# Layer 1 causal attention of a two-layer decoder: when the later-token value sums are made

## The chip, the cores and the metric

The kernel runs on one core of a Trainium2 chip. The metric is the device time of one execution in microseconds (us); the time before is 1584.54 us, the median of three runs.

## The reference, cut to what matters

A post-norm decoder of two layers works on `x` of 4 batches x 512 tokens x 512 features, in float32. Each layer is a self-attention, a cross-attention and a feed-forward, each added to `x` and layer-normalized. The change is in the self-attention of layer 1 (16 heads of 32 features):

```python
kqv = x @ Wqkv + bqkv                      # (b, s, 3, 16, 32): q, k, v
scores = einsum('bsnh,btnh->bnst', k, q) / sqrt(32)
scores = triu(scores) + -10000.0 * tril(ones, k=-1)
attn = softmax(scores, axis=2)
out = einsum('bnkq,bknh->bqnh', attn, v)
out = out @ Wo + bo
```

The masked places are not left out: the score there is -10000, not minus infinity. So each row's result is the sum over the tokens up to it, plus a factor exp(-10000 - row maximum) times the plain sum of the values of all later tokens. That plain sum depends on `v` alone, and one matrix of 128 x 512 for each of the four tiles of 128 tokens holds it for all 16 heads. These are the later-token value sums.

## The kernel before

**Stages and lanes.** Six phases are written as Python generators: A, B, C (attention, cross-attention and feed-forward of layer 0) and D, E, F (of layer 1), each for batches 0 to 3. `lanes` keeps two generators alive and steps them in turn; a generator ends a step with `yield`. A generator can say "next", after which the next one of the order A0 A1 ... F3 may start beside it. D says so at head 8 (`hh == D_NEXT`, 7), so D1 starts while D0 does heads 9 to 16. Weight preparation runs as background generators beside given stages (`BESIDE`); beside D1 to D3 this is the unpacking of the feed-forward's 4-bit codes (L1074, L1075, L1082 on VectorE, 22 tiles).

**Deferred steps.** Inside a generator, `pipe.later(n, f)` puts off `f` by n ticks, and each step begins with `pipe.tick()`. So while head `hh` has its scores made, head `hh-1` has its softmax and head `hh-2` its transposes.

**The order on the engines.** The Tile framework takes the traced program, gives each instruction a priority by its place in the code, and a planner with its own model of durations writes the queue of each engine; an instruction that is ready by that model can pass an earlier one that isn't. Semaphores and buffers are assigned by it. A buffer of a pool is given to a tile at its first write and comes back after its last reader; a tile that finds none waits.

**Pools.** `self.op` ("o") has 69 buffers of 128 x 512 float32 and holds weights, values, stacked queries and keys and most other results; `tp` ("t") has 13 for short-lived tiles; PSUM has 8 banks under one tag.

**One batch of D** (`l1_attn`), with float32 values split into a high and a low part where a product needs three passes (`mm3`, L154 to L156):
- Steps 0 to 7: load `x`, transpose it (L248) and split it into `xT` (`dxh`, `dxl`: 8 tiles of "o").
- `project(w, m)`: 12 matmuls to one bank (`dq`) give queries (w = 0) or keys (w = 1) of the four heads 4m+1 to 4m+4. `pair` evacuates (ScalarE, L840, L842), rounds (ScalarE, L844) and makes the low part (GpSimd, L845). `stack` loads four "o" tiles `stk` (L853), each with three DMAs, two from SyncE's queue and one from GpSimd's. The projections of m = 0 come before the values, the others at heads 1, 2 / 5, 6 / 9, 10.
- Four steps of values: 12 matmuls each into `dv`; `values` keeps `dv` and its two parts `dvh`, `dvl` (12 tiles of "o" in all).
- Sixteen head steps: `scores` (L908, four matmuls of one head from its two `stk`), `soft` (VectorE L919, ScalarE L923), `turn` (transposes L933, copies L942 to `dpT`), and behind every fourth head `values_out` (L953, matmuls `do` from ten `dpT` tiles) and `keep_out` (L958).
- `later_sum(i)`: for token tile i, matmuls (L894) of the constant 0/1 matrices `upto` and `after` with `dvh` and `dvl`. All four sums accumulate in one PSUM bank, from tile 3 down to tile 0; after each, `keep_sum` copies the bank to an "o" tile `suf[i]` (ScalarE, L899).
- Behind the heads: `suf[i]` is scaled (GpSimd, L989) and added to the turned outputs (VectorE, L983, L984), the result is transposed (`dF`), multiplied by `Wo` (`dy`), added and normalized.

In the code heads are counted from 0 (`hh`); the text counts them from 1. D0 to D3 are the four batches of this phase.

Of the kernel before, what the change touches and what calls it, by code (L numbers as in the profile page):

```python
# [23 lines left out]
NT = 4  # L24
# [44 lines left out]
class Net:  # L69
# [750 lines left out]
    def l1_attn(self, b):  # L820
# [11 lines left out]
        def project(w, m):  # L832
            ps = self.pa("dq")
            self.mm3(ps, [(self.cols(self.w1[k, w], slice(m * P, (m + 1) * P)), xT[k]) for k in range(NT)])
            pipe.later(1, pair, w, m, ps)
# [49 lines left out]
        def later_sum(i):  # L885


            if not later:
                later.append(self.pb("suf"))
            ps = later[0]  # L890
            todo = [(self.upto, r) for r in vp[i + 1]] if i + 1 < NT else []
            todo += [(self.after, r) for r in vp[i]]
            for n, (l, r) in enumerate(todo):
                nc.tensor.matmul(ps, l, r, start=i + 1 == NT and n == 0, stop=n == len(todo) - 1, skip_group_check=True)  # L894
            pipe.later(1, keep_sum, i, ps)
# [5 lines left out]
        def scores(hh):  # L901
            q3, k3 = st.pop((0, hh)), st.pop((1, hh))
            p01, p2, p3 = self.pa("ds"), self.pa("ds"), self.pa("ds")
            place = ((p01, 0), (p01, 256), (p2, 0), (p3, 0))
            tiles = []
            for i, (ps, o) in enumerate(place):
                w = max(256, P * (i + 1))
                nc.tensor.matmul(ps[:, o : o + w], q3[:, i * P : (i + 1) * P], k3[:, 0:w], start=True, stop=True, skip_group_check=True)  # L908
                tiles.append(ps[:, o : o + P * (i + 1)])
            pipe.later(1, soft, hh, tiles)  # L910
# [50 lines left out]
        for hh in range(16):  # L961
            pipe.tick()
            if hh % 4 < 2 and hh < 12:
                project(hh % 4, hh // 4 + 1)
            if hh < 4:
                later_sum(NT - 1 - hh)
            scores(hh)
            yield "next" if hh == D_NEXT else None
        yield from pipe.drain()
# [400 lines left out]
```

## Time and profile before

| what | value |
|---|---|
| runs | 1584.54 us median of 3 (1584.25 to 1585.16) |
| profiled execution | 1581.65 us, span 1580.0 us |
| mean granted TensorE clock | 0.996 |
| TensorE / VectorE / ScalarE / GpSimd busy | 1515.4 / 1232.9 / 1021.3 / 666.2 us |
| first and last later-sum matmul | 775.7 and 1076.4 us |

First score matmul of a head (L908; four of them belong to one head), in us from the start of the span:

| batch | head 1 | head 5 | head 9 | head 13 | head 16 |
|---|---|---|---|---|---|
| D0 | 776.1 | 792.6 | 808.0 | 821.2 | 831.5 |
| D1 | 859.3 | 878.4 | 898.0 | 918.6 | 929.0 |
| D2 | 974.6 | 993.3 | 1008.8 | 1022.7 | 1033.9 |
| D3 | 1061.5 | 1078.5 | 1097.6 | 1117.7 | 1128.1 |

How to read the profile: PE is the matmul part of TensorE, PEld its weight loads, DVE is VectorE, ACT ScalarE, POOL GpSimd, SP SyncE, and a q behind a name is that engine's queue (its sequencer). L894 is line 894 of the kernel. A row `a <- b` says that a waited and that b ended the wait. A tile is named without its number, and `out<-in` says what an instruction writes and reads. Matmuls overlap, so the busy time of PE is no measure of its work; the distance between the starts of two matmuls in a row is.

### The profile page before, as it was taken

Reading aid. Unit: us, or ns where it says so; the run is one execution under the profiler, and the core shown is the slowest. Engines: PE = TensorE matmul, PEld = TensorE weight load, DVE = VectorE, ACT = ScalarE, POOL = GpSimd, SP = SyncE. Lnnn points to the kernel's source line nnn. Section 1 sums busy time; section 2 is a strip of 40 time slices with the busy share of each in tenths; the row PEclk is TensorE's granted clock in tenths of the full one; section 3 lists DMA queues with packets and bytes.
Section 4 is the critical chain, followed back from the end, with each engine's and each line's share of the span. In section 5 each row is a group of like instructions: output and inputs, shape, how many; then the busy total and the mean of one; then the engine's idle time right before and its main releaser. Section 6 shows DMA issues by size and latency. Waiting matters only on the chain.

```text
span 1580.0 us, 25595 instructions
## 1 busy us (share of the span) xinstructions
PE 1515.4 (96%) x8222; PEld 1090.1 (69%) x8222; DVE 1232.9 (78%) x2658; ACT 1021.3 (65%) x2208; POOL 666.2 (42%) x672
## 2 busy tenths in 40 slices
PE   8999999999999999899999999999999999999996
PEld 6888786444544674477777668777687777777875
DVE  6486589999976688777577797767786888888896
ACT  5333336988878877888696864969634445545554
POOL 6673663555535303430435323353225344344342
PEclk9999999999999999999999999999999999999998
DMA  7043344455214744653434445633436630020101
GB/s 255 29 157 124 113 154 132 149 173 176 78 48 123 224 137 133 201 185 134 134 102 118 104 141 148 171 97 92 125 123 222 233 110 12 24 81 1 54 1 53
DMA packets 134150, 192.31 MB, mean 122 GB/s; under 512 B 17265, under 2 KB 52081, under 8 KB 134017
## 3 DMA queue, kind: packets, MB, share of 16 engines
q1 hardware_dynamic: 129888, 182.23, 36.3%
q0 software_dynamic: 4128, 8.46, 2.2%
q8 instruction: 65, 1.06, 0.3%
q14 instruction: 69, 0.56, 0.1%
HBM read 117.75 MB, written 47.71 MB: 105 GB/s over the span
## 4 chain that ended last, share of the span: by engine, by line
PE 63%; DVE 17%; ACT 8%; issue 6%; DMA 3%; POOL 3%; SPq 0%; ACTq 0%; DVEq 0%; POOLq 0%
PE fg L1185 7%; PE facc L1168 5%; PE dT L933 3%; DVE fg L1141 3%; PE pg L687 3%; PE had L755 2%; PE dn L741 2%; DVE bsm L474 2%; PE pu L689 2%; ACT de L923 2%; PE bo L498 2%; PE do L953 2%; PE qk L156 2%; PE qk L155 2%; PE qk L154 2%
## 5 line engine op out<-in xcount | busy, mean ns | idle before, releaser
L1141 DVE SCALAR_TENSOR_TENSOR fg<-fg,gs,fg 128x512 f32<-128x512 f32 x220 | 163.2, 745 | 30.9 <-ACT fg L1133 15.3
L923 ACT ACTIVATE de<-de,dm 128x128 f32<-128x128 f32 (+3 forms) x256 | 142.9, 563 | 11.3 <-DVE dm L919 10.9
L1185 PE MATMUL fg<-fxh,gu 128*128 128x512 f32 x352 | 140.2, 398 | 6.1 <-DVE fg L1141 3.1
L919 DVE CUSTOM_DVE_ANT_0 de<-ds,negm,thr 128x128 f32<-128x128 f32 (+3 forms) x256 | 126.4, 546 | 19.4 <-PE ds L908 16.0
L482 POOL TENSOR_SCALAR be<-be,bsm 128x512 f32<-128x512 f32 x128 | 96.5, 766 | 103.8 <-DVE bsm L480 72.7
L1185 PE MATMUL fg<-fxl,gu 128*128 128x512 f32 x352 | 137.4, 390 | 0.1
L664 POOL TENSOR_TENSOR hl<-g,hh 128x512 fp32r<-128x512 f32 x64 | 83.4, 1309 | 110.2 <-ACT hh L663 90.2
L1145 POOL TENSOR_TENSOR fg<-fg,fg 128x512 f32<-128x512 f32 x44 | 60.2, 1367 | 139.6 <-DVE fg L1141 60.0
L476 ACT ACTIVATE be<-bs,bsm 128x512 f32<-128x512 f32 x128 | 87.3, 690 | 31.1 <-DVE bsm L474 29.2
L845 POOL TENSOR_TENSOR dql<-dqf,dqh 128x512 fp32r<-128x512 f32 x32 | 41.4, 1295 | 150.8 <-ACT dqh L844 150.6
L933 PE MATMUL dT<-ident,de 128*128 128x128 f32 x640 | 92.0, 280 | 8.5 <-ACT de L923 6.4
L933 PEld LDWEIGHTS dT<-ident,de 128*128 128x128 f32 x640 | 72.3, 142 | 28.3 <-ACT de L923 14.0
L1185 PEld LDWEIGHTS fg<-fxh,gu 128*128 128x128 f32 x352 | 66.0, 188 | 30.1 <-DVE fg L1141 12.7
L474 DVE TENSOR_REDUCE bsm<-bs 128x1 f32<-128x512 f32 x128 | 83.4, 672 | 0.0
L498 PE MATMUL bo<-bpT,cT 128*64 128x512 f32 x256 | 76.7, 618 | 2.4 <-ACT bpT L489 1.2
L248 PEld LDWEIGHTS bT<-ident,be 128*128 128x128 f32 x512 | 54.9, 141 | 34.0 <-issue 11.5
L248 PE MATMUL bT<-ident,be 128*128 128x128 f32 x512 | 73.2, 281 | 3.6 <-POOL be L482 2.1
L1185 PEld LDWEIGHTS fg<-fxl,gu 128*128 128x128 f32 x352 | 66.1, 188 | 12.8 <-DVE fxl L146 0.4
L352 POOL TENSOR_TENSOR z<-z,rope_cos 128x512 f32<-128x512 f32 x32 | 46.8, 1473 | 64.8 <-DVE zs L349 57.8
L1133 ACT ACTIVATE fg<-fg,gs 128x512 f32<-128x512 f32 x88 | 60.1, 684 | 20.6 <-PE fg L1185 20.4
L687 PE MATMUL pg<-qT,tb 128*128 128x512 bf16 x256 | 66.8, 381 | 4.5 <-ACT qT L649 2.8
L1159 POOL TENSOR_TENSOR fhl<-fg,fhh 128x512 fp32r<-128x512 f32 x44 | 58.5, 1331 | 29.5 <-ACT fhh L1158 29.3
(355 smaller groups left out, 4640.3 us busy)
## 6 DMA issues: line engine op xcount, KB each, us to landing
x<-x SPq DMA_DIRECT2D x176, 256.0 KB, 3.0
had_scratch<-hw SPq DMA_DIRECT2D x64, 256.0 KB, 2.3
z<-had_scratch SPq DMA_DIRECT2D x64, 256.0 KB, 5.8
stk<-dqh SPq DMA_DIRECT2D x192, 64.0 KB, 2.1
tw<-in_wg_t SPq DMA_DIRECT2D x32, 256.0 KB, 3.8
tw<-in_wu_t SPq DMA_DIRECT2D x32, 256.0 KB, 3.7
tw<-in_wd_t SPq DMA_DIRECT2D x32, 256.0 KB, 2.8
p<-in_gu_p SPq DMA_DIRECT2D x22, 256.0 KB, 3.1
```

The costliest lines, as they stand in the source:

```text
L248: self.nc.tensor.transpose(pt[:, i * P : (i + 1) * P], srcs[i][:, j * P : (j + 1) * P], self.ident)
L474: nc.vector.tensor_reduce(sm[:, h : h + 1], ps, AX.X, ALU.max, negate=True)
L476: nc.scalar.activation(e, ps, AF.Exp, bias=sm[:, h : h + 1], accum_out=sm[:, 2 + h : 3 + h])
L482: nc.gpsimd.tensor_scalar(es[h][i], es[h][i], sm[:, 4 + h : 5 + h], 1.0, ALU.mult, ALU.mult)
L498: nc.tensor.matmul(po[0][h * 64 : h * 64 + 64, :], cT[j][:, c : c + 64], pTs[h], start=j == 0, stop=j == NT - 1)
L664: nc.gpsimd.tensor_tensor(lo, g, hi.bitcast(F32), ALU.subtract)
L687: nc.tensor.matmul(pg, tern["wg_t"][k, c][:, m], qT[k], start=k == 0, stop=k == NT - 1)
L919: nc.vector.tensor_tensor_reduce(es[i], ps, self.negm[:, 384 - P * i :], -1.0, self.thr[:, i : i + 1], ALU.add, ALU.min, n4[:, i : i + 1])
L923: nc.scalar.activation(es[i], es[i], AF.Exp, bias=n4[:, i : i + 1], scale=-1.0, accum_out=den[:, hh * 4 + i : hh * 4 + i + 1])
L933: nc.tensor.transpose(pt[:, o + (i - j) * P : o + (i - j + 1) * P], es[i][:, j * P : (j + 1) * P], self.ident)
L1141: self.emitted["DVE"] = nc.vector.scalar_tensor_tensor(y[u], ps, s, y[u], ALU.mult, ALU.add)
L1185: nc.tensor.matmul(ps, self.gu[i, u][:, g * P : (g + 1) * P], xT[g][n], start=n == 0, stop=n == 1)
```

## The change

The four calls of `later_sum` move from the steps of heads 1 to 4 to those of heads 13 to 16, in each of the four batches. The order of the four sums stays: tile 3 first, tile 0 last. The call still stands ahead of the head's `scores`.

```diff
@@ -962,8 +962,9 @@
             pipe.tick()
             if hh % 4 < 2 and hh < 12:
                 project(hh % 4, hh // 4 + 1)
-            if hh < 4:
-                later_sum(NT - 1 - hh)
+
+            if hh >= 12:
+                later_sum(15 - hh)
             scores(hh)
             yield "next" if hh == D_NEXT else None
         yield from pipe.drain()
```

## The prediction

> **What bounds the kernel now.** I read the page first, then the later sums' own instructions, then the engines' busy time in the attention heads, then SyncE's queue and the chain of waits.
>
> The page's engine line and its chain say that TensorE carries most of the kernel, but not alone:
>
> ```profile
> PE 1515.4 (96%) x8222; PEld 1090.1 (69%) x8222; DVE 1232.9 (78%) x2658; ACT 1021.3 (65%) x2208; POOL 666.2 (42%) x672
> ...
> PE 63%; DVE 17%; ACT 8%; issue 6%; DMA 3%; POOL 3%; SPq 0%; ACTq 0%; DVEq 0%; POOLq 0%
> ```
>
> These are averages over six stages. The change lives in the fourth, from about 775 to 1140 us, so it is priced there. The view of the tile `suf` gives what is moved: x16 and x12 are counts over the four batches, then min/median/max in ns.
>
> ```profile
> L894 PE MATMUL suf<-dvh,after x16: 388/393/396, 775.7 to 1076.2; 128*128 128x512 f32 x16
> L894 PE MATMUL suf<-dvl,after x16: 389/393/403, 775.9 to 1076.4; 128*128 128x512 f32 x16
> L899 ACT COPY suf<-suf x16: 568/582/601, 776.5 to 1077.3; 128x512 f32<-128x512 f32 x16
> L989 POOL TENSOR_TENSOR suf<-suf,dm x16: 1066/1084/1549, 844.4 to 1137.6; 128x512 f32<-128x512 f32 x16
> ```
>
> Next the busy time, in stretches from the first score matmul (L908) of head 1 to that of head 5, and from that of head 13 to 5 us behind that of head 16. Columns: stretch, length, then PE, PEld, DVE, ACT, POOL busy us (with counts), granted clock, DMA share, GB/s. Four rows for heads 1 to 4 of D0 to D3, then four for heads 13 to 16.
>
> ```profile
> 776.10:792.60 16.50, 15.52 (x84) 12.25 (x84) 9.60 (x35) 16.16 (x45) 6.49 (x10) 1.00 0.39 98
> 859.30:878.40 19.10, 17.15 (x90) 13.00 (x89) 16.04 (x46) 15.63 (x44) 6.43 (x10) 1.00 0.44 117
> 974.60:993.30 18.70, 18.59 (x95) 14.47 (x94) 15.07 (x49) 15.62 (x46) 6.57 (x10) 1.00 0.62 186
> 1061.50:1078.50 17.00, 16.45 (x88) 12.77 (x87) 14.69 (x45) 15.44 (x44) 6.62 (x10) 1.00 0.37 93
> 821.20:836.50 15.30, 14.68 (x109) 10.66 (x110) 14.28 (x44) 15.30 (x47) 5.01 (x4) 1.00 0.22 73
> 918.60:934.00 15.40, 13.72 (x106) 10.06 (x105) 15.35 (x53) 12.83 (x41) 0.00 (x0) 1.00 0.21 69
> 1022.70:1038.90 16.20, 14.32 (x113) 10.51 (x112) 14.77 (x45) 16.20 (x50) 5.00 (x4) 1.00 0.20 60
> 1117.70:1133.10 15.40, 13.87 (x106) 10.09 (x105) 13.84 (x49) 13.06 (x41) 0.00 (x0) 0.98 0.02 5
> ```
>
> The reader is to see that the last four heads are not free. In D0 and D2 ScalarE is busy without a gap there (15.30 of 15.30, 16.20 of 16.20); in D1 VectorE is (15.35 of 15.40). TensorE alone has room.
>
> Last, what SyncE's queue waits for in batch D1 (858 to 940 us; total, times, longest), and then the chain of waits there (start, length, what):
>
> ```profile
> SPq L853 <- PE do L953: 10.8, 1, 10.8
> ```
>
> ```profile
> 884.31 2.29 PE do L953 x32
> ```
>
> L853 loads the stacked queries and keys of heads to come. Its next load is issued at 885.32, after 10.8 us of waiting, just behind the first value matmuls (`do`, L953) of heads 1 to 4 at 884.31. Those read the transposed probabilities `dpT`, and with them ten buffers of the pool "o" come free. So the loads wait for buffers.
>
> **The change part by part.**
>
> *What moves.* For each batch 2+4+4+4 = 14 matmuls and 4 ScalarE copies. Successive L894 rows of the timeline start 0.23 us apart (775.69, 775.92), so 14 x 0.23 = 3.2 us of TensorE; 4 x 0.582 = 2.3 us of ScalarE. Nothing is added, no DMA moves, and SyncE and GpSimd get no new instruction. One PSUM bank is held during heads 13 to 16 instead of 1 to 4.
>
> *Heads 1 to 4, relieved.* In D0 ScalarE is 16.16 of 16.50 busy, so its 2.3 us come off. In D1 ten of the 14 matmuls stand in gapless TensorE stretches (860.9 to 867 and 874.6 to 878.4), 10 x 0.23 = 2.3. In D2 (TensorE 18.59 of 18.70) and D3 (ScalarE 15.44, TensorE 16.45 of 17.00) I take 2.3 too; a batch's bounds are 1 and 3.2. Sum: -9.2 (-4 to -12.8).
>
> *Heads 13 to 16, loaded.* In D0 and D2 the four copies go to a full ScalarE: +2.3 each (bounds 0, if other copies fall back behind VectorE, and 3.2). The matmuls fit in TensorE's gaps there. In D1 VectorE is full and gets nothing; TensorE runs without a gap only in heads 13 and 14, where 2+4 matmuls cost 6 x 0.23 = 1.4 (0 to 3.2). In D3 nothing runs beside the tail: the same 1.4, plus the two copies of heads 15 and 16, 1.2, in a chain that is ScalarE's exponentials from 1127 to 1132 us: 2.6 (0 to 5.5). Sum: 2.3 + 2.3 + 1.4 + 2.6 = +8.6 (0 to 15).
>
> So the move itself is a swap, -0.6 us.
>
> [...]
>
> *New waits.* All four sums share a bank, so each waits for the copy of the one before. Before, TensorE and its loads waited 2.6 us in 7 times for that. Behind such a matmul stands the next head's score group, for which VectorE and then ScalarE wait. With ScalarE full its copy comes later, but one head keeps ScalarE 3.8 us (15.3/4) while scores and first reduction take about 1 us (0.65 + 0.35), so it should not starve: 0 taken, up to +3 in all. GpSimd's L989 now reads sums that are made last; the earliest of D0 runs at 844.4, while D0's last scores are out by 834. The copy of sum 0 is due about one head later (3.8 us), so 6 us cover it; GpSimd's additions, splits and stack loads for the next batch queue behind it if not.
>
> *The pool "o", 69 buffers.* This is the term that decides. Today the eight tiles `dvh`, `dvl` end in heads 1 to 4, and four `suf` tiles begin. After the change all eight live on to heads 13 to 16 and no `suf` exists until then: from head 4 to 13 four buffers more are held. I count who holds one in D1 at 881.5 us, just ahead of the first value matmuls, from first write to last read in the trace: 32 weight pairs and 1 bias, 8 of `xT`, 4 of `v`, 4 `suf`, 6 stacks still unread, 10 `dpT`, 4 `do` of D0's merge = 69. It is exactly full. With 73 wanted, the value matmuls, which need all ten `dpT`, must wait until four buffers come back; the score matmuls give two a head, so for two heads' scores, of which today one is out in time (883.2) and the next comes 4.5 us later (887.6). What then is late: the stack loads of heads 9 to 12 behind it on SyncE (16 issues, 885.3 to 895.4) and D0's `dF` splits.
>
> How much of that is paid? Later scores can be drawn forward, so nothing is a floor (a gain has no reason: buffers only get fewer); twice a head's 4.5 us is the ceiling, 9. The nearest row is what the full pool costs already. By the usual spacing of each shape (0.226 us for 512 columns, 0.109 for 128, 0.072 for L953) TensorE's work in heads 5 to 8 is 16.4 us of D1's 19.6 and 14.7 of D0's 15.4. D1 idles about 3.3 us; I take as much again: +3.3. D0 and D2 have no merge beside heads 1 to 4; the same count reaches 69 in head 5, and four more overflow for some 3 us, mostly stacks with 4 us to spare: +0.4 each (0 to 2). In D3 eight weight buffers are free already (63 at most): 0. Sum: +4.1 (0 to 13).
>
> [...]
>
> **The sum.** -9.2 + 8.6 + 4.1 = +3.5 us. The profiled execution took 1581.65 us (span 1580.0 and 1.65 around it), 2.9 below the median of the runs; the terms are differences, so I put them on the median: 1584.54 + 3.5 = 1588.0. About 0.2%, 3.2 us, is what a measurement of this kernel can tell from no change.
>
> **The rivals.**
> - *The cover holds* (faster). If the last heads' ScalarE is elastic and the planner draws scores forward so that the pool never stalls TensorE, the relief of 9.2 meets only D1's and D3's 4.0: -5 us, 1579.5. For it: TensorE's gaps in heads 13 to 16. Against it: ScalarE without one gap in D0 and D2. It decides if the late copies cost less than half (under 2.3 of 4.6) and D1's heads 5 to 8 stay at 19.6 us.
> - *Nothing nets* (same). The planner orders by its own idea of ready; the moved matmuls depend only on the values, and if it pulls them forward into gaps they end early and free the pool. Then the change does not quite do what it says: about +0.5, 1585. For it: L894 already wanders by a group in the timeline (in the middle of a projection at 875.9). Against: TensorE's order follows the code almost everywhere in these heads.
> - *The pool at its ceiling* (slower). Both value groups of D1 stall, 9 us, and D0 and D2 pay 2 each: -0.6 + 13 = +12.4, 1597.
>
> **How the numbers follow.** The pool deciding, at 1585.5 to 1597, has 0.55 of chance, 0.49 of it over 3.2 us; nothing netting 0.24; the cover holding 0.21. Faster 0.22 (nearly all of the last, a little of the second), same 0.28, slower 0.50. The range, 1581 to 1597, leaves out the tail below -3.5 and a little above the ceiling; the likeliest case's own is 1585.5 to 1597.
>
> **What would show each step.** Right: heads 1 to 4 shorter by about 2.3 us a batch; heads 13 to 16 of D0 and D2 longer by as much with ScalarE gapless; in D1 the first `do` group later against its first head than today's 25.0 us (884.31 less 859.3), scores of heads 6 and 7 ahead of it, SyncE's longest wait above 10.8, heads 5 to 8 above 19.6. Wrong: L894 rows long before head 13; D1's heads 5 to 8 unchanged; or the main difference outside 775 to 1140 us, which would mean that the planner's order elsewhere changed and none of these terms decided.

## The result, and the profile after

The changed kernel takes 1607.55 us (median of 4 runs, 1606.6 to 1610.14) against 1584.39 before: 1.0152 times, interval 1.0135 to 1.0169, some 23 us slower. 1588.0 was predicted, with a range up to 1597. The profiled executions have spans of 1605.8 and 1580.0 us, so 25.8 us are to be found.

The page's engine line after:

```profile
PE 1526.6 (95%) x8191; PEld 1096.8 (68%) x8222; DVE 1234.8 (77%) x2658; ACT 1022.8 (64%) x2208; POOL 666.7 (42%) x672
```

Against 1515.4, 1090.1, 1232.9, 1021.3 and 666.2 little grew but TensorE's own time, its matmuls by 11.2 us and its weight loads by 6.7, and that is less than half of the loss. (The page has 31 matmul records fewer, though the weight loads are 8222 as before: records are missing.) So it is mostly waiting. The tile `suf` shows that the change did what it says: nothing was pulled forward, the first sum runs at 820.8 us.

```profile
L894 PE MATMUL suf<-dvh,after x16: 392/397/502, 820.8 to 1152.2; 128*128 128x512 f32 x16
L894 PE MATMUL suf<-dvl,after x16: 388/394/399, 821.1 to 1152.4; 128*128 128x512 f32 x16
L899 ACT COPY suf<-suf x16: 590/593/623, 825.9 to 1153.5; 128x512 f32<-128x512 f32 x16
L990 POOL TENSOR_TENSOR suf<-suf,dm x16: 1072/1090/1537, 846.5 to 1159.4; 128x512 f32<-128x512 f32 x16
```

Where the time went is read from the first score matmul of a head to that of another, after less before (us; predicted in the last column):

| stretch | D0 | D1 | D2 | D3 | sum | predicted |
|---|---|---|---|---|---|---|
| head 1 to 5 | -1.8 | -2.2 | -1.9 | -2.2 | -8.1 | -9.2 |
| head 5 to 13 | +3.3 | +14.5 | +3.4 | +0.5 | +21.7 | +4.1 |
| head 13 to 16 | +2.5 | +3.1 | +1.7 | +3.0 | +10.3 | +8.6 |
| between the batches | | | | | -2.2 | 0 |
| behind D3's head 16 | | | | | +4.1 | 0 |

In D1 the stretch from head 5 to 13 goes from 40.2 to 54.7 us. Its busy time, first before, then after (stretch, length, then PE, PEld, DVE, ACT, POOL busy us with counts, granted clock, DMA share, GB/s):

```profile
878.40:918.60 40.20, 38.36 (x264) 29.91 (x262) 29.65 (x92) 32.69 (x90) 13.08 (x20) 1.00 0.42 113
```

```profile
879.70:934.40 54.70, 44.55 (x267) 32.17 (x266) 32.20 (x94) 34.34 (x92) 13.06 (x20) 0.94 0.30 77
```

The work is the same. Before, TensorE is busy in 38.36 of 40.20 us; after, it stands idle for 10.15 of 54.70, no other engine is full, and the granted clock is 0.94. The queue of SyncE after, in D1, 860 to 960 us (total, times, longest):

```profile
SPq L853 <- PE do L953: 17.5, 3, 14.8
SPq L853 <- PE ds L908: 14.1, 4, 13.1
```

The wait for the value matmuls grew from 10.8 to 14.8 us, and a second of 13.1 us, for score matmuls, has come. Both are stack loads that wait for a buffer of "o". TensorE's timeline shows the worst place (start, length, what; in brackets how long TensorE stood idle before it, and who ended that):

```profile
906.50 0.51 PE L908 MATMUL ds<-stk,stk 96*128 96x256 f32 x2 [0.84 <-ACT dqf L840]
910.10 0.66 PE L908 MATMUL ds<-stk,stk 96*128 96x384 f32 x1 [3.09 <-DVE dm L919]
911.48 0.79 PE L908 MATMUL ds<-stk,stk 96*128 96x512 f32 x1 [0.72 <-DVE dm L919]
913.05 1.97 PE L933 MATMUL dT<-ident,de 128*128 128x128 f32 x8 [0.79 <-DVE dpT L942]
914.67 0.78 PE L154 MATMUL dq<-dxh,w1h 128*128 128x512 f32 x1
```

The four score matmuls of head 9, which need 0.65 us in a row, take from 906.50 to 912.27: the first two go when ScalarE has emptied the bank of a projection, each of the others when VectorE has read an earlier bank of scores. By a count of who holds a buffer, "o" is full from 873 to about 890 us and again from 898 to 919, with some room for 8 us behind the first value matmuls, and it gets none back between 902 and 912. VectorE's timeline in the same place:

```profile
907.93 0.79 DVE L1075 TENSOR_SCALAR p<-p,i 128x512 int32<-128x512 int32 x1 [6.83 <-DMA p<-in_gu_p]
...
909.17 0.35 DVE L919 CUSTOM_DVE_ANT_0 de<-ds,negm,thr 128x128 f32<-128x128 f32 x1
...
912.31 0.69 DVE L942 COPY dpT<-dT 128x512 f32<-128x512 f32 x1 [0.89 <-PE ds L908]
```

Head 8's transposes sit in PSUM, since no buffer is free to copy them to: the copy at 912.31 goes when head 9's last score matmul has given its stacks back. Head 9's scores meanwhile must pass through the banks that are left. So pool and PSUM hold each other; this is read from the waits, and no experiment tests it alone. A second path adds to it. The load of a tile of 4-bit codes stands behind the late stack loads in SyncE's queue (issued at 904.73); VectorE waits 6.83 us for it, and so it reads head 9's first scores at 909.17, some 2 us after they were made. From 858 to 945 us VectorE's waits for these loads are 0.6 us before and 6.8 after, 0.9 in experiment 1 and 10.0 in experiment 5 below.

The projection behind head 9 (914.67) then starts its matmuls 0.58 and 0.42 us apart, not 0.23: the granted clock is 0.50 for 6.8 us from 909.2.

### The profile page after: what moved, and what is told of

It is laid out like the page before. It is cut to its first block, busy times and chain, and to the rows that moved or that the text cites. A ratio compares the mean times of both kernels' runs of the same rounds, so it can differ in the third digit from the quotient of the medians.

```text
span 1605.8 us, 25573 instructions
## 1 busy us (share of the span) xinstructions
PE 1526.6 (95%) x8191; PEld 1096.8 (68%) x8222; DVE 1234.8 (77%) x2658; ACT 1022.8 (64%) x2208; POOL 666.7 (42%) x672
## 5 line engine op out<-in xcount | busy, mean ns | idle before, releaser
L1142 DVE SCALAR_TENSOR_TENSOR fg<-fg,gs,fg 128x512 f32<-128x512 f32 x220 | 163.1, 745 | 31.0 <-ACT fg L1134 15.6
L248 PEld LDWEIGHTS bT<-ident,be 128*128 128x128 f32 x512 | 55.0, 141 | 34.0 <-issue 11.9
L1186 PEld LDWEIGHTS fg<-fxl,gu 128*128 128x128 f32 x352 | 66.1, 188 | 12.8 <-DVE fxl L146 0.4
L908 PE MATMUL ds<-stk,stk 96*128 96x256 f32 (+2 forms) x256 | 62.2, 350 | 10.0 <-DVE dm L919 3.8
```

The source lines that it names most:

```text
L248: self.nc.tensor.transpose(pt[:, i * P : (i + 1) * P], srcs[i][:, j * P : (j + 1) * P], self.ident)
L1142: self.emitted["DVE"] = nc.vector.scalar_tensor_tensor(y[u], ps, s, y[u], ALU.mult, ALU.add)
L1186: nc.tensor.matmul(ps, self.gu[i, u][:, g * P : (g + 1) * P], xT[g][n], start=n == 0, stop=n == 1)
```

## The experiments

Theory P: the four buffers that are held longer cost the middle heads. Rival L: the late sums cost wherever they stand, by their own time or by the order that they bring. Each comparison is with runs of before on the same chip (medians 1579.66, 1582.04 and 1582.14 us in the three sets), so the ratios count. Stretches are head 1 to 5, 5 to 13, 13 to 16, in us.

**1. The change without the held buffers.** `dvl` goes to another pool.

```diff
-            f, hi, lo = self.o("dv"), self.o("dvh", F32R), self.o("dvl", F32R)
+            f, hi, lo = self.o("dv"), self.o("dvh", F32R), self.sb(self.xp, "x", "dvl", F32R, 512)
```

> The changed kernel, but the four low parts of the values (dvl) of each batch stand in the pool of the x tiles, which has four buffers to spare in these stages, so the pool o has its four buffers back in heads 5 to 13. If the missing buffers are the cause (theory P), heads 5 to 12 of D1 go from 54.7 us back to about 40, those of D0 and D2 from 31.9 and 32.8 to about 29, SyncE's waits of 14.8 and 13.1 us in D1 fall back to some 11, and the time is 1584.4 plus the swap's own cost, 3 to 6 us: 1587 to 1591. If the late work itself is the cause (theory L: full ScalarE and the later scores in heads 13 to 16 throw back everything), it stays at 1604 to 1608. If any new order of the planner costs that much (theory O), it lies anywhere from 1585 to 1610 and D1's heads 5 to 12 do not come back.

Measured: 1590.41 us, 1.0076 (1.0063 to 1.0089). D1 is 14.9, 41.0, 13.5; D0's and D2's middle 30.4 and 31.0, from 32.0 and 32.8. The row of D1's middle:

```profile
875.60:916.60 41.00, 39.16 (x268) 30.58 (x267) 30.50 (x93) 33.08 (x90) 13.03 (x20) 1.00 0.44 118
```

TensorE is full again and the clock whole. Half of the loss is gone; the rest, 0.76%, has nothing to do with these four buffers.

**2. The same edit in the kernel before**, as a control.

> The kernel before, with the same four low parts in the pool of the x tiles: the control of the run above, and a try for a faster version. Theory P: the pool o was exactly full in heads 5 to 9 of D1 before, so some of D1's 3.3 us of idle TensorE there may go: 1581 to 1585. Theory L: no change, 1583.5 to 1585.5. Theory O: anywhere within 10 us of 1584.

Measured: 1581.34 us, 1.0013 (1.0004 to 1.0022). D1's heads 1 to 4 are 2.1 us shorter, and as much is lost elsewhere. The other pool is no gift in itself.

**3. Four idle buffers held in the kernel before.**

```diff
+            if hh == 4:
+                held = [self.o("held") for _ in range(4)]
+            if hh in (4, 12):
+                for f in held:
+                    nc.gpsimd.memset(f[:, 0:1], 0.0)
```

> The kernel before, with the sums still beside heads 1 to 4, but from head 5 to head 13 of each batch four buffers of the pool o are held by idle tiles (a one-column memset on GpSimd takes each, another gives it back; 32 small memsets in all). Theory P: the loss without the move, D1's heads 5 to 12 longer by 10 to 16 us, D0's and D2's by 2 to 4 each, D3's by nothing, 1600 to 1607 in all. Theory L: 1584 to 1586, since nothing is moved. Theory O: no particular place.

Measured: 1581.02 us, 1.0007 (0.9997 to 1.0017), D1's middle 40.2. It looks like a blow to P and is none. GpSimd's timeline in D1:

```profile
878.64 1.20 POOL L971 MEMSET held<- 128x1 f32 x8 [6.08 <-DVE do L988]
```

All eight writes, the four that take and the four that should give back at head 13, stand in one row of 1.20 us: the second four wait for nothing. The buffers were not held. Experiment 5 mends that.

**4. The change in D3 alone.**

```diff
-            if hh >= 12:
-                later_sum(15 - hh)
+            if (hh >= 12) if b == 3 else (hh < 4):
+                later_sum(NT - 1 - hh % 4)
```

> The move in the last batch (D3) alone, where the pool has buffers to spare (63 of 69 at most): the swap by itself. Theory P: heads 1 to 4 shorter by about 2 us, the tail (heads 13 to 16 and what follows up to the cross-attention) longer by 4 to 7: 1586.5 to 1589.5. Theory L: a fourth of the whole loss, about 6 us, 1590, with D3's heads 13 to 16 as its place. Theory O: anywhere.

Measured: 1585.31 us, 1.0044 (1.0031 to 1.0058), some 6 to 7 us over before. That is above theory P's 2 to 5 and near theory L's 6, but L's place for it was heads 13 to 16, where only 3.0 us stand. D3 is 15.6, 39.7, 13.4 against 17.0, 39.2, 10.4: -1.4, +0.5, +3.0. Behind head 16 it loses 3.5 us more, in E0's start, with a half-clock spell of 10.2 us there, from 1146.2 (experiment 6).

**5. The held buffers without the change.** The sums stay; a late access keeps `dvl`.

```diff
+            if hh >= 12:
+                nc.vector.tensor_copy(vp[15 - hh][1][:, 0:1], n4[:, 3:4])
```

> The sums stay at heads 1 to 4 as before; only the four dvl tiles of each batch live on to heads 13 to 16, because VectorE writes one column of them there from that head's row minima (16 copies of 128x1 more, well under 0.1 us each). So the pool holds as many tiles in heads 5 to 12 as with the change, and nothing else of the change is made. Theory P (the held buffers are the loss in heads 5 to 12, the place of the sums is not): D1 heads 5 to 12 take 50 to 55 us instead of 40.2, D0 and D2 2 to 4 us more than 28.7 and 29.4, heads 1 to 4 and 13 to 16 stay at 19.1 and 10.4 in D1; in all 1594 to 1602 us. Rival L (the loss in the middle heads comes from an order of the queues that only late sums bring): D1 heads 5 to 12 at 40 to 42, in all 1579 to 1583.

Measured: 1601.76 us, 1.0119 (1.0098 to 1.0141). D1 is 18.1, 56.1, 10.4. The middle and the same place on TensorE:

```profile
879.90:936.00 56.10, 46.01 (x267) 33.16 (x266) 31.38 (x93) 34.30 (x93) 13.04 (x20) 0.91 0.29 72
```

```profile
907.37 0.51 PE L908 MATMUL ds<-stk,stk 96*128 96x256 f32 x2 [0.84 <-ACT dqf L840]
910.97 0.66 PE L908 MATMUL ds<-stk,stk 96*128 96x384 f32 x1 [3.09 <-DVE dm L919]
912.35 0.80 PE L908 MATMUL ds<-stk,stk 96*128 96x512 f32 x1 [0.72 <-DVE dm L919]
913.93 1.97 PE L935 MATMUL dT<-ident,de 128*128 128x128 f32 x8 [0.79 <-DVE dpT L944]
```

It is the same stall, gap for gap, with every sum in its old place. P is shown: the buffers alone make D1's middle what it is after the change. A new order of the queues as such (theory O) does not: experiment 2 has one too, and its D1 middle is 40.5 us. (The sixteen added copies took 0.146 us each, more than expected, but they stand at heads 13 to 16.) The two halves, 1.19% here and 0.76% in experiment 1, are together more than the change's 1.52%, so the shares are not exact: D1's middle takes 56.1 us here at a clock of 0.91, after the change 54.7 at 0.94.

**6. D3 alone, with TensorE kept busy behind it.**

```diff
+        if b == 0:
+            fil = self.pa("fil")
+            for _ in range(38):
+                nc.tensor.transpose(fil[:, 0:P], x[NT - 1][:, 0:P], self.ident)
```

> The change in D3 alone (1585.31 against 1579.66 before, with a half-clock spell of TensorE from 1146.2 us for 10.2 us), and 38 transposes of 128x128 into an unread PSUM bank just behind E0's own transposes of x, about 38 x 0.109 = 4.1 us, where TensorE stands idle (1143.7 to 1147.9). Theory C (the idle time brings the half clock, and the half clock makes E0's first products late): no spell near 1146, the es products start 0.23 us apart from the first on, 15 of them 0.2 us shorter each: 2.5 to 3.5 us less than 1585.3, so 1582 to 1583. Rival T (E0 is late because its loads are late, the clock costs nothing): 1585 to 1586, spell or not. Rival F (the filler itself is in the way of dF and es): over 1586.

Without the filler (experiment 4), then with it:

```profile
1147.91 0.79 PE L154 MATMUL es<-ecTh,exh 128*128 128x512 f32 x1 [2.76 <-DVE exl L146]
1148.50 0.63 PE L155 MATMUL es<-ecTl,exh 128*128 128x512 f32 x1
1148.93 0.63 PE L156 MATMUL es<-ecTh,exl 128*128 128x512 f32 x1
```

```profile
1143.11 4.37 PE L1037 MATMUL fil<-ident,x 128*128 128x128 f32 x38 [0.49 <-DVE do L984]
...
1148.57 0.47 PE L154 MATMUL es<-ecTh,exh 128*128 128x512 f32 x1
1148.87 0.39 PE L155 MATMUL es<-ecTl,exh 128*128 128x512 f32 x1
1149.10 0.40 PE L156 MATMUL es<-ecTh,exl 128*128 128x512 f32 x1
```

The spell is gone and the products start 0.23 us apart, not 0.42. Yet the whole took 1588.35 us, 1.0041 (1.0029 to 1.0052): nothing won. At 6.3 us over before this is the case of rivals T and F, not theory C's 2 to 3. E0's products begin 1.8 us later after head 16 (17.9 against 16.1), and another half-clock spell, 6.8 us at 1264, falls on the start of F0. So with TensorE's idle time filled the spell was gone, as theory C has it; its price is not settled.

**7. Thin late sums.** Experiment 1 with one matmul a sum.

```diff
             todo += [(self.after, r) for r in vp[i]]
+            todo = todo[:1]
```

> The change with dvl in the pool x (1590.41), and each of the four late sums made of one matmul instead of two or four: 10 of 14 matmuls a batch are left out, so the later-token sums are incomplete; the four copies of each batch stay. It tells which engine pays in heads 13 to 16. Theory M (TensorE's time, 0.23 us a matmul): heads 13 to 16 fall by about 2.3 us in D1 and D3 (13.5 and 13.4 to about 11.2), by 1 to 2 in D0 and D2, in all 1582 to 1587. Rival S (the ScalarE copies and the wait on the one bank, as the prediction had it for D0 and D2): heads 13 to 16 within 0.5 us of 12.8, 13.5, 12.9, 13.4, in all 1589 to 1591.

Measured: 1580.25 us, 0.9987 (0.9969 to 1.0004). Heads 13 to 16 take 12.6, 11.9, 11.6, 12.1 us, from 12.8, 13.5, 12.9, 13.4; behind head 16 there is neither loss nor spell. The ten matmuls left out paid 1.3 to 1.6 us a batch in D1 to D3, under the 2.3 expected. In D0 it is 0.2, but a half-clock spell of 3.4 us, from 822.9, falls into its heads 13 and 14. In all that is 4.4 of the 10.3 us that these heads cost. The other 5.9 stay with the four matmuls, the four copies and the waits on the one bank that each batch keeps, so the matmuls are a large part of the price and the copies are not cleared of the rest. The whole fell by more, from 1.0076 to 0.9987, some 14 us where 4 to 8 were expected.

**8. The sums where TensorE has gaps**: at heads 7, 9, 11, 15, copies on VectorE, `dvl` as in experiment 1.

```diff
-            if hh < 4:
-                later_sum(NT - 1 - hh)
+            if hh in (6, 8, 10, 14):
+                later_sum({6: 3, 8: 2, 10: 1, 14: 0}[hh])
```

> A version to beat both: the four sums of each batch at heads 7, 9, 11 and 15, where TensorE's work by usual spacing fills about half of the head before (0.47 to 0.68 of it), their copies on VectorE (busy 0.6 to 0.75 of heads 6 and 10) instead of ScalarE, and dvl in the pool x so that the pool o holds no more than before. Theory (places with room on TensorE and VectorE and no held buffer cost nearly nothing): heads 1 to 4 shorter by about 2 us a batch, 8 in all, heads 5 to 16 longer by 2 to 5 in all, 1574 to 1578. Rival (the middle heads have no real room, since the next head's scores wait in line behind each sum): the gain is given back, 1579 to 1585.

Measured: 1589.2 us, 1.0041 (1.0027 to 1.0055), slower than before; the rival's case, a little beyond it. Heads 1 to 4 gain 9.4 in all (14.6, 14.8, 16.8, 15.6), the middle gives 13.6 back (33.0, 43.3, 33.0, 41.8) and heads 13 to 16 another 1.3. A gap on TensorE between two heads was not room here; whether the matmuls or their copies on VectorE took more than it held is not separated.

**9. Two buffers short instead of four.**

```diff
-            f, hi, lo = self.o("dv"), self.o("dvh", F32R), self.o("dvl", F32R)
+            f, hi, lo = self.o("dv"), self.o("dvh", F32R), self.o("dvl", F32R) if len(v) % 2 else self.sb(self.xp, "x", "dvl", F32R, 512)
```

> The change with two of the four dvl tiles of each batch in the pool x: the pool o is short by two buffers in heads 5 to 12, not by four. D1 heads 5 to 12 took 41.0 us at none short and 54.7 at four. Theory linear (each buffer has its price): 46 to 49 us, in all about 14 to 18 us over before. Theory lock (the price comes when the score matmuls of two heads more are needed to free four stacks, and the transposes of those heads in turn find no buffer for dpT; two buffers come back with one head): 41 to 44 us, in all 7 to 11 us over before.

Measured: 1600.13 us, 1.0118 (1.0088 to 1.0147). D1's middle:

```profile
877.20:924.50 47.30, 42.39 (x268) 32.60 (x267) 31.94 (x93) 33.13 (x90) 12.94 (x20) 0.93 0.39 100
```

41.0, 47.3 and 54.7 us at none, two and four short: some 3.4 us a buffer, near a straight line. Part of it is the clock: 0.93 of 47.3 us, 0.94 of 54.7 and 0.91 of 56.1 are 3.3, 3.3 and 5.0 us of full clock missing, the most that the spells can have cost there. Less that, 41.0, 44.0 and 51.4 are left, and 44.0 is also the upper end of theory lock. So two buffers do cost something, but whether the price is a line or a step stays open.

**10 and 11. Value matmuls behind every second head**, in the kernel after and in the one before, to give the buffers back in smaller lots.

```diff
-            if hh % 4 == 3:
-                pipe.later(1, values_out, cur[:])
+            if hh % 2:
+                pipe.later(1, values_out, hh, cur[:])
...
-            po = self.pb("do")
+            po = two.pop() if hh % 4 == 3 else self.pb("do")
```

> The change, and the value matmuls (L953) run behind every second head instead of every fourth, into the same bank of four heads: five dpT tiles come back two heads earlier, and no more than five or so wait at a time. Nothing is left out. Theory P with the lock (pool and PSUM hold each other because ten dpT must exist before any comes back): D1 heads 5 to 12 fall from 54.7 to 41 to 45 us, and D0, D2 from 32.0 and 32.8 to about 30.5 and 31; in all 6 to 11 us over before. Rival (what is short is buffers as such, in whatever order they come back): D1 stays above 48 us, in all over 14 us slower than before.

> The kernel before, with the value matmuls behind every second head: a version to beat both. Theory (the full pool already costs in before: SyncE's 10.8 us wait at D1's first value group, TensorE's idle 3.3 us in D1's heads 5 to 8): D1 heads 5 to 12 fall from 40.2 to 36 to 39 us, D0 and D2 by up to 1, in all 2 to 5 us faster than before. Rival B (TensorE's other work bounds these heads, and the bank of do is held two heads longer): D1 39 to 41, in all within 2 us of before or up to 4 slower.

Measured: 1643.4 us, 1.0386 (1.0363 to 1.0408), and 1632.25, 1.0319 (1.0295 to 1.0343). Both are far slower, for a reason that none of the theories had. A value group before, then one of half the size in experiment 11:

```profile
884.24 2.36 PE L953 MATMUL do<-dpT,dv 128*32 128x512 f32 x32
```

```profile
934.70 2.35 PE L955 MATMUL do<-dpT,dv 128*32 128x512 f32 x16
```

32 matmuls of four heads (the trace has two rows for each matmul of the code) take as long as 16 of two, 2.36 us against 2.35. As I read it, those whose results lie in different 32-partition parts of the bank ran side by side. Twice as many groups are 4 x 2.35 = 9.4 us more a batch, 38 of the 50 us. So D1's 48.6 us in experiment 10 is beyond the 48 that was to speak for the rival, but the yardstick moved: against 44.4 in experiment 11 the change costs 4.2 there, not 14.5. That fits the lock of pool and PSUM and does not prove it.

**12. The copies of the sums on VectorE** in D0 and D2 of the kernel before.

```diff
-            nc.scalar.copy(suf[i], ps)
+            (nc.vector.tensor_copy if b in (0, 2) else nc.scalar.copy)(suf[i], ps)
```

> The kernel before, with the four copies of the sums (L899, 0.582 us each on ScalarE) on VectorE in D0 and D2, where ScalarE is busy 16.16 of 16.50 and 15.62 of 18.70 us in heads 1 to 4 and VectorE 9.60 and 15.07. Theory S (ScalarE sets the pace in D0's first heads, as the prediction had it): D0 heads 1 to 4 fall from 16.4 to 14 to 15 us, D2 by 0 to 1, in all 1 to 3 us faster. Rival M (TensorE's matmuls pay there, the copies ride along): D0 at 16 to 17, D2 at 18 to 19, in all within 1.5 us of before.

Measured: 1581.24 us, 0.9996 (0.9987 to 1.0006), no difference. D0's heads 1 to 4:

```profile
777.00:793.20 16.20, 15.83 (x83) 12.31 (x82) 12.11 (x39) 14.50 (x41) 6.47 (x10) 1.00 0.41 103
```

ScalarE fell from 16.16 to 14.50 us of work, and the stretch, by its head starts, from 16.4 to 16.2. ScalarE was full there and did not set the pace. TensorE, at 15.83 of 16.20, is the engine that stays full.

## Why the prediction was wrong

**The step that failed is the pool's price.** The prediction found the place (D1, exactly full at 881.5 us), the cause (four buffers more held), and the sign; experiments 1 and 5 bear all three out. It put +3.3 on D1 with 9 as the ceiling; D1 lost 14.5, of which 13.7 went with the buffers (54.7 less 41.0). The ceiling allowed two events, a head's 4.5 us for each of the two value groups in these heads. The first was sized well: that group starts at 889.50 instead of 884.24, 3.9 us late beyond the 1.4 that D1 already lagged at head 5. The second was not: 921.70 instead of 906.26, 14.0 us late by the same count. Two things were missing. The shortage goes on after the first group: the pool is full again from 898 to 919 us, and D1's lag grows from head 5 to head 10 (+1.4 at head 5, +6.2 at 7, +8.5 at 9, +15.4 at 10). And at head 9 the wait runs through PSUM and VectorE's queue, where a head's scores took 5.8 us instead of 0.65; the sum had no term for that, nor for the half clock behind it, which is at most 3.3 us of the 13.7. D0 and D2, priced at 0.4, lost 3.3 and 3.4, of which 1.6 and 1.8 were the buffers. D3, priced at 0, lost 0.5: right.

**Heads 1 to 4, relieved: right in size, in D0 wrong in reason.** -8.1 against -9.2. But the prediction took ScalarE's 2.3 us off in D0; experiment 12 takes those copies away and gains 0.2. That leaves the matmuls: twelve of the 14, 2.8 us, stand in this stretch (the first sum's two run just ahead of head 1's scores), and about 2 us of it came off. In D1 the prediction put ten matmuls into its two gapless stretches; the timeline has eight there, 1.8 us, and 2.2 came off.

**Heads 13 to 16, loaded: +10.3 against +8.6, with the engine in large part mistaken.** The four rows after, from head 13 to 5 us behind head 16, D0 to D3:

```profile
822.50:840.30 17.80, 17.61 (x117) 12.52 (x118) 15.19 (x46) 16.03 (x46) 5.00 (x4) 1.00 0.18 61
934.40:952.90 18.50, 18.22 (x124) 12.82 (x122) 16.93 (x56) 15.27 (x45) 0.00 (x0) 1.00 0.27 91
1041.30:1059.20 17.90, 17.55 (x117) 12.50 (x118) 15.13 (x46) 16.02 (x46) 5.00 (x4) 1.00 0.13 45
1136.30:1154.70 18.40, 18.11 (x124) 12.81 (x123) 14.88 (x51) 14.57 (x44) 0.00 (x0) 1.00 0.13 47
```

Now TensorE is full in all four, ScalarE in none. The prediction read "TensorE alone has room" from 13.7 to 14.7 busy us in 15.3 to 16.2. As I read it, that room was the wait between two heads, in which TensorE's next work was not ready; a sum put ahead of the scores pushes the whole chain behind it. Experiment 7 gives ten of the 14 matmuls 4.4 of the 10.3 us and leaves 5.9 undivided between the other four, the copies and the shared bank; experiment 8 finds no room in such gaps elsewhere.

**The swap is therefore +5 rather than -0.6** without the buffers: in experiment 1 the three stretches sum to -10.1 + 4.6 + 10.3.

**What was not in the sum: 4.1 us behind D3's last head.** TensorE after, in E0's start:

```profile
1159.00:1164.00 5.00, 3.00 (x24) 2.50 (x23) 2.31 (x4) 1.03 (x2) 1.45 (x2) 1.00 0.91 320
1164.00:1169.00 5.00, 2.90 (x8) 2.02 (x8) 3.61 (x5) 3.77 (x8) 4.75 (x4) 0.62 0.55 170
1169.00:1174.00 5.00, 4.80 (x17) 3.68 (x17) 5.00 (x9) 0.00 (x0) 0.92 (x1) 0.70 0.81 307
```

E0's context loads land 6.0 to 7.3 us after issue instead of 3.3 to 5.7. ScalarE holds in order the rounding of those loads, for which it waits 3.9 us, and of E0's own rows, so TensorE stands still (2.6 us until the first `exl`); then the granted clock is 0.50 from 1165.2 to 1172.0 us, while it has a backlog. The sums' tail gives that its chance: such a loss is there when all of D3's sums are late and whole (3.6 us in experiment 1, 3.9 in 4, 5.9 in 9) and absent with thin ones (7) or held buffers alone (5). The profile of before has a short spell of its own there, 3.4 us from 1132.5, so 4.1 is rather too little. How much is the loads and how much the clock stays open.

Of the rivals "the pool at its ceiling" was nearest. Its mechanism decided; its ceiling did not hold. "The cover holds" fell with D1's heads, "nothing nets" with the first `suf` at 820.8.

No version tried is faster than before by a difference that can be measured. Experiments 8, 11 and 12 were aimed at that.

## What to carry to other kernels

When a change keeps tiles alive longer in a pool that is already full, do not price it as one late event: follow the shortage until the pool has slack again, and ask which other resource the blocked tiles sit in meanwhile. A test of it is cheap, since a late dummy access holds a tile without moving any work, but look in the trace whether it does hold. Do not count the idle time of an engine between two steps of a chain as room for work that stands ahead of the chain's next step: here such moves gave back all that they had won.

## What the runs showed of the hardware

**Half-clock spells.** TensorE's granted clock fell to 0.50 for 3.4 us (before, from 1132.5), for 6.8 (after, from 909.2) and for 10.2 (experiment 4, from 1146.2). In a stretch as long as the shortest of them, 3.4 us, ahead of the spell in D1 after, and ahead of the one from 1132.5 in before:

```profile
905.80:909.20 3.40, 0.51 (x2) 0.30 (x2) 1.24 (x3) 1.27 (x2) 1.25 (x1) 1.00 0.52 154
```

```profile
1129.10:1132.50 3.40, 1.87 (x12) 1.04 (x10) 3.40 (x13) 3.37 (x11) 0.00 (x0) 0.99 0.00 0
```

TensorE was 0.15 and 0.55 busy, and its longest idle stretch there 2.19 and 0.74 us. So these spells came without TensorE being fully idle ahead of them. Nor does its busy time decide it: from 496.8 to 500.2 us of before TensorE is 1.51 us busy, less than the 1.87 ahead of 1132.5, and the granted clock stays at 1.00. What sets a spell off stays open. Among the executions of the kernel before in the second set, the two with a mean clock of 0.998 took 1578.4 and 1580.2 us, the two with 0.994 1584.7 and 1588.0: some 1.8 us for each 0.001, and one spell of 3.4 us takes 1.7/1580 = 0.0011 from the mean. So a stall with a spell behind it is paid twice, as in D1 after: 3.09 us of idle TensorE, then a projection's matmuls 0.42 us apart instead of 0.23.

**Four matmuls side by side.** 32 value matmuls in 2.36 us against 16 in 2.35 is a factor of 2.0 in matmuls per time, with four 32-partition parts of the bank instead of two.
